# Reordering layer 0's products in the second slot and moving the next element's left sums to the third

## The chip, the cores and the metric

The kernel runs on one NeuronCore of a Trainium2 chip. The metric is the device time of one execution in microseconds (us), the median of several. The names in the profile: PE is TensorE's matmuls and PEld its weight loads, DVE is VectorE, ACT is ScalarE, POOL is GpSimd, SP is the engine that issues the DMAs. L547 is line 547 of the kernel before.

## The reference

For each of 64 elements (256 rows of 512 numbers, fp32), two layers one after the other, each with a residual and a layer norm:

```python
# layer 0: a graph layer
mi = x @ Wi.T;  mj = x @ Wj.T                 # W = [Wi | Wj]
x = layernorm(x + deg * (mi + b) + a @ mj)    # a = adjacency (256 x 256), deg = its row sums
# layer 1: attention over the graph, 8 heads of 64
q, k, v = x @ Wq.T + bq, x @ Wk.T + bk, x @ Wv.T + bv
scores = where(adj == 0, -inf, q @ k.T / 8)
x = layernorm(x + (softmax(scores) @ v) @ Wo.T + bo)
```

## The kernel before

**Products.** The two weight products of layer 0 and the four of layer 1 are done with seven block products in place of eight (a Strassen-like scheme). Its left operands are four quarters of the input and four sums or differences of them (S1 to S4, "left sums", made by `left_steps`, lines 477 to 480); its right operands are quarters of the weights and their differences, made once. For layer 0 `l0_steps(b)` returns the work of element b as a list: seven products `step1` to `step7` (called first to seventh product here, `p[0]` to `p[6]` in the lists), then the product with the graph (`neighbours`), then the layer norm and the transfer of the result (`take`, `give`, `send_h`). A product is two matmuls in the program, four in the records, onto one PSUM bank. Some products share a bank: x takes the first and third, y the fourth and sixth, z the fifth and seventh.

- Product 4 goes to y; VectorE reads it and makes u2 = y + u1 (L542).
- Product 5 goes to z; ScalarE copies z to half of mj (L547).
- Product 6 adds into y; VectorE makes u3 = y + u1 (L551); GpSimd adds u3 to that half of mj (L552), and `split` makes hi (ScalarE, L524) and lo (GpSimd, L525) of it. VectorE also adds deg * u3 to the residual (L520).
- Product 7 adds into z, so it may not start before ScalarE's copy of z is over; VectorE makes the other half of mj from z and u2 (L561), which is split in the same way.

**Elements and slots.** Two elements (b1, b2) make a group. The main loop runs 31 times; in a pass the attention of group g is interleaved with layer 0 of group g+1. `layer0(g + 1)` returns seven lists, `work[0]` to `work[6]`, and the loop runs each at a place of its own between the attention's products; the diff's "second slot" is `work[1]`, its "third slot" `work[3]`, behind the scores of head pair 5. In order of time, a pass is: `work[0]`; values of head pairs 0 and 1, their denominators (`divide_two`: den and the reciprocal rden, L882), scores of 2 and 3, **`work[1]`**; values of 2 and 3, denominators, scores of 4, `work[2]` (the graph product of b1), scores of 5, **`work[3]`**; values of 4 and 5, denominators, scores of 6 and 7, `work[4]` (products 4 to 7 of b2); values of 6 and 7, and the output and query/key/value products.

After each scores product VectorE adds the mask (L805), ScalarE takes the exponential (L809), and GpSimd adds the halves for the denominators (L812).

**What sets the order.** Matmuls, and all that stands in `in_order(...)`, are pinned behind what was written before them on the same engine; the rest is placed by the framework's scheduler, by program order where it expects the inputs to be ready. The left sums of layer 0 (`sum_x`) are pinned; the mask addition, the scaled additions L520 and the reciprocal L882 aren't. The four left sums of an element share one buffer (xS, one copy), so those of b2 can be written only when product 7 of b1 has read S4. The banks of layer 0's products and of den come from one pool of three.

Of the kernel before, what the change touches and what calls it, by code (L numbers as in the profile page):

```python
# [9 lines left out]
F32R = mybir.dt.float32r  # L10
I32 = mybir.dt.int32
AF = mybir.ActivationFunctionType
ALU = mybir.AluOpType
# [3 lines left out]
P = 128  # L17
# [207 lines left out]
def unshifted_path(ctx, tc, flag, x, adj, wiT, wjT, b0, wqT, bq, wkT, bk, wvT, bv, woT, bo, out):  # L225
# [16 lines left out]
    nc = tc.nc  # L242
    B, N, D = x.shape
    NT = N // P
# [12 lines left out]
    p1 = ctx.enter_context(tc.tile_pool(name="p1", bufs=1))  # L257
# [11 lines left out]
    def bank(name):  # L269
        return ps_m.tile([P, 512], F32, tag="mm", name=name)  # L270

    def score_banks(name):
        return ps_s.tile([P, 2, 512], F32, tag="sc", name=name)
# [8 lines left out]
    def in_order(ins):  # L282

        tc.keep_in_program_order(ins)
# [4 lines left out]
    def matmul(*args, **kw):  # L289
        in_order(nc.tensor.matmul(*args, **kw))  # L290
# [160 lines left out]
    def norm_stats(t, order=anywhere):  # L451
        st = small.tile([P, 6], F32, tag="st", name="st")
        order(nc.vector.bn_stats(st, t))
        mv = small.tile([P, 2], F32, tag="mv", name="mv")
        nc.vector.bn_aggr(mv, st)
        ve = small.tile([P, 1], F32, tag="ve", name="ve")
        nc.vector.tensor_scalar(ve, mv[:, 1:2], EPS, None, ALU.add)
        below = small.tile([P, 1], F32, tag="below", name="below")
        order(nc.vector.tensor_scalar(below, mv[:, 0:1], -1.0, None, ALU.mult))  # L459
        rstd = small.tile([P, 1], F32, tag="rstd", name="rstd")  # L460
        nc.gpsimd.tensor_tensor(rstd, ve, mhalf, ALU.pow)  # L461
        return below, rstd

    def norm_apply(t, below, rstd, order=anywhere):
        shift = small.tile([P, 1], F32, tag="shift", name="shift")
        order(nc.scalar.activation(shift, below, AF.Identity, scale=rstd))  # L466
        order(nc.scalar.activation(t, t, AF.Identity, bias=shift, scale=rstd))  # L467
# [34 lines left out]
    def l0_steps(b):  # L502
        banks, k = {}, {}

        def product(name, left, n, first):
            if first:
                banks[name] = bank("po")
            for c in range(2):
                matmul(banks[name], left[:, c, :], w0[:, n, c, :], start=(first and c == 0),
                                 stop=(c == 1), skip_group_check=True)  # L510

        def raw(t, h):
            return xT[b][:, 2 * h:2 * h + 2, t * P:(t + 1) * P]

        def keeper(name):
            k[name] = p3.tile([P, D], F32, tag="lu", name=name)
            return k[name]

        def add_scaled(t, src):
            nc.vector.scalar_tensor_tensor(xh[b][:, t, :], src, deg[:, t:t + 1], xh[b][:, t, :],  # L520
                                           ALU.mult, ALU.add)

        def split(t):
            nc.scalar.copy(k["hi"][:, t, :], k["mj"][:, t, :])  # L524
            nc.gpsimd.tensor_tensor(k["lo"][:, t, :], k["mj"][:, t, :], k["hi"][:, t, :].bitcast(F32),  # L525
                                    ALU.subtract)

        def step1():
            product("x", raw(0, 0), B11, True)
            nc.scalar.copy(keeper("u1"), banks["x"])  # L530

        def step2():
            product("w", raw(1, 1), T4, True)
            add_scaled(1, banks["w"])

        def step3():
            product("x", raw(0, 1), B21, False)
            add_scaled(0, banks["x"])

        def step4():  # L540
            product("y", xS[b]["S2"], T2, True)
            nc.vector.tensor_add(keeper("u2"), banks["y"], k["u1"])  # L542

        def step5():
            product("z", xS[b]["S1"], T1, True)
            k["mj"] = p1.tile([P, NT, D], F32, tag="mj", name="mj")
            nc.scalar.copy(k["mj"][:, 1, :], banks["z"])  # L547

        def step6():
            product("y", xS[b]["S3"], T3, False)  # L550
            nc.vector.tensor_add(keeper("u3"), banks["y"], k["u1"])  # L551
            nc.gpsimd.tensor_tensor(k["mj"][:, 1, :], k["mj"][:, 1, :], k["u3"], ALU.add)  # L552

            k["hi"] = p1.tile([P, NT, D], F32R, tag="hi", name="hi")
            k["lo"] = p1.tile([P, NT, D], F32R, tag="lo", name="lo")
            split(1)
            add_scaled(1, k["u3"])

        def step7():
            product("z", xS[b]["S4"], B22, False)  # L560
            nc.vector.tensor_add(k["mj"][:, 0, :], banks["z"], k["u2"])  # L561
            split(0)

        stats = {}

        def neighbours():
            k["pa"] = score_banks("pa")
            for i in (1, 0):
                for n, (j, part) in enumerate((j, part) for j in (1, 0) for part in ("hi", "lo")):
                    matmul(k["pa"][:, i, :], graph[:, j, i * P:(i + 1) * P], k[part][:, j, :],  # L570
                           start=(n == 0), stop=(n == 2 * NT - 1))

        def take(t):
            r = xh[b][:, t, :]
            in_order(nc.vector.tensor_add(r, k["pa"][:, t, :], r))
            stats[t] = norm_stats(r, in_order)

        def give(t):
            norm_apply(xh[b][:, t, :], *stats[t], in_order)


        return [step1, step2, step3, step4, step5, step6, step7, neighbours, lambda: take(1), lambda: take(0),
                lambda: give(1), lambda: send_h(b, 1), lambda: give(0), lambda: send_h(b, 0)]

# [10 lines left out]
    def send_h(b, t):  # L595
        i = b % NB
        if t == 1:
            h_cols[b] = dram.tile([D // P, N, P], F32, tag=f"h{i}", name="h_cols")
        nc.sync.dma_start(out=h_cols[b][:, t * P:(t + 1) * P, :].rearrange("q p n -> p q n"),
                          in_=xh[b][:, t, :].rearrange("p (q n) -> p q n", n=P))  # L600
        if t == 0:
            hB[b] = p1.tile([P, N // R, P], F32, tag="hB", name="hB")
            nc.sync.dma_start(out=hB[b].rearrange("p a n -> p (a n)"),
                              in_=h_cols[b].rearrange("q (r a) n -> (q r) (a n)", r=R))
# [63 lines left out]
    def second_late(steps):  # L668
        return [steps[0], steps[2], steps[1], *steps[3:]]
# [30 lines left out]
    def qk_steps(g, store, tag, bias, diff, early=False):  # L700

        def new_store():
            store[g] = p1.tile([P, NC, NB * N], F32, tag=tag, name=tag)

        def place(i, j):
            return store[g][:, 2 * j:2 * j + 2, i * N:(i + 1) * N]

        def biased(b):
            def evict(dst, ps):
                for m in range(2):  # L710
                    nc.scalar.activation(dst[:, m, :], ps[:, m, :], AF.Identity, bias=b[:, m:m + 1], scale=1.0)  # L711
            return evict

        def last(dst, ps, addend):
            for m in range(2):
                nc.vector.scalar_tensor_tensor(dst[:, m, :], ps[:, m, :], diff[:, m:m + 1],
                                               addend[:, m, :], ALU.add, ALU.add)

        return qkv_steps(g, True, new_store, place, biased(bias), biased(diff), last, early)
# [175 lines left out]
    def layer0(g):  # L895

        b1, b2 = NB * g, NB * g + 1

        def item(f, *args):
            return lambda: f(*args)  # L900

        p, q = l0_steps(b1), l0_steps(b2)
        return [p[:3] + [item(turn_x, b2)] + p[3:4],
                p[4:7] + [item(sum_x, b2), item(add_bias, b2)] + q[:1],
                p[7:10], p[10:] + q[1:3],
                q[3:6] + [item(turn_h, b1)] + q[6:7],
                q[7:], [item(turn_h, b2)]]

# [4 lines left out]
    def with_output_bias(g, k):  # L913
        return [*k[:2], lambda: add_output_bias(NB * g), k[2], lambda: add_output_bias(NB * g + 1), *k[3:]]

    def order_of(name):
        return [(name, n) for n in RIGHT]

    for g in range(-1, NG - 1):
        o, q, k, v = (order_of(name) for name in ("wo", "wq", "wk", "wv"))  # L920
# [18 lines left out]
    p, q = l0_steps(0), l0_steps(1)  # L939
# [19 lines left out]
    k = second_late(qk_steps(0, kT, "kT", bk_sb, bkd, True))  # L959
# [22 lines left out]
    for g in range(NG - 1):  # L982
# [20 lines left out]
        q = second_late(qk_steps(g + 1, qT, "qT", bq_sb, bqd))  # L1003
        k = second_late(qk_steps(g + 1, kT, "kT", bk_sb, bkd, True))
# [7 lines left out]
        k = with_output_bias(g + 1, k)[2:]  # L1012
# [101 lines left out]
```

## Time and profile before

The median of 3 runs is 3117.14 us (3116.6 to 3118.32); the profiled execution has a span of 3113.4 us at a granted TensorE clock of 0.999.

| engine | busy us | share of the span |
|---|---|---|
| PE (matmul) | 3071.3 | 99% |
| PEld (weight loads) | 2117.8 | 68% |
| DVE | 2148.5 | 69% |
| POOL | 1520.8 | 49% |
| ACT | 1007.8 | 32% |

A row of the order in time gives the start (us into the span), the length, engine, line, operation, what is written and read, the shapes, how many instructions the row merges, and in brackets how long the engine had been idle and what ended that. "issue" there means that the engine waited for nothing that the profile shows. In the list of waits a row gives who waited for whom, the total in us, how often, and the longest. A matmul's end is modelled, so a gap on TensorE is better read from the starts of its weight loads.

### The profile page before, as it was taken

The page shows a single profiled execution, that of the slowest core. Times are in us where ns is not written, and L with a number is a line of the kernel's source. Part 1 is how long each engine was busy: PE and PEld are TensorE (multiplying, and loading weights), DVE is VectorE, ACT ScalarE, POOL GpSimd, SP SyncE. Part 2 cuts the span into 40 slices and gives each one's busy share as a digit, 9 for nine tenths or more (in the row PEclk, how much of TensorE's full clock was granted, in tenths as well). Part 3 has the DMA queues.
Part 4 walks back from the last instruction along what each step waited for, and adds up shares of the span by engine and source line. Part 5 has one row for each costly group of instructions (what it writes and reads, how often), then busy time and mean ns, then how long its engine had stood idle before and what let it go on. Part 6 is the DMA issues. An engine that isn't in the chain of part 4 may idle for free. (4 is left out here: it accounts for less than half of the span.)

```text
span 3113.4 us, 42777 instructions
## 1 busy us (share of the span) xinstructions
PE 3071.3 (99%) x14598; PEld 2117.8 (68%) x14598; DVE 2148.5 (69%) x3234; ACT 1007.8 (32%) x1925; POOL 1520.8 (49%) x1255
## 2 busy tenths in 40 slices
PE   7999999999999999999999999999999999999998
PEld 5667766677766677666776667766677766677665
DVE  6776676766777667676667676667766667767665
ACT  2333333323333333333233332333333333323332
POOL 2544445544545445454454554454544546445453
PEclk9999999999999999999999999999999999999999
DMA  7345544455444555445553445544455444555333
GB/s 256 121 143 156 166 124 134 128 157 165 141 124 123 157 166 152 117 131 149 157 166 118 131 134 157 165 139 123 127 155 169 146 118 127 154 162 160 116 111 98
DMA packets 410395, 447.28 MB, mean 144 GB/s; under 512 B 40896, under 2 KB 300224, under 8 KB 409792
## 3 DMA queue, kind: packets, MB, share of 16 engines
q1 hardware_dynamic: 410176, 444.50, 48.3%
q8 instruction: 120, 1.97, 0.3%
q14 instruction: 99, 0.81, 0.1%
HBM read 340.79 MB, written 70.25 MB: 132 GB/s over the span
## 5 line engine op out<-in xcount | busy, mean ns | idle before, releaser
L461 POOL TENSOR_TENSOR rstd<-ve,mhalf 128x1 f32<-128x1 f32 x256 | 140.6, 554 | 724.3 <-DVE below L459 724.3
L812 POOL TENSOR_TENSOR pk<-pe 128x512 f32<-128x512 f32 x256 | 322.3, 1275 | 341.0 <-ACT pe L809 341.0
L290 PE MATMUL po<-w,xS 128*128 128x512 f32 x1024 | 470.4, 602 | 6.1 <-ACT mj L547 5.6
L290 PE MATMUL st<-hS,factor 128*128 128x256 f32 x2048 | 452.7, 379 | 1.2 <-DVE u L685 1.2
L290 PEld LDWEIGHTS st<-hS,factor 128*128 128x128 f32 x2048 | 388.4, 190 | 55.1 <-DVE u L685 1.6
L809 ACT ACTIVATE pe<-pe 128x1024 f32<-128x1024 f32 x256 | 270.8, 1058 | 379.2 <-DVE pe L805 379.2
L290 PE MATMUL st<-hT,factor 128*128 128x256 f32 x1536 | 360.7, 381 | 9.0 <-ACT u L711 8.4
L290 PE MATMUL po<-w,xT 128*128 128x512 f32 x768 | 352.3, 601 | 13.8 <-DVE xT L485 11.3
L290 PEld LDWEIGHTS po<-w,xS 128*128 128x128 f32 x1024 | 186.8, 190 | 252.2 <-issue 191.5
L290 PEld LDWEIGHTS st<-hT,factor 128*128 128x128 f32 x1536 | 289.0, 190 | 61.5 <-ACT u L711 20.8
L805 DVE TENSOR_TENSOR pe<-ps,maskT 128x1024 f32<-128x1024 f32 x256 | 297.8, 1194 | 35.3 <-PE ps L290 35.3
L882 DVE RECIPROCAL rden<-den 128x256 f32<-128x256 f32 x127 | 222.8, 1754 | 73.7 <-PE den L290 68.2
L290 PEld LDWEIGHTS po<-w,xT 128*128 128x128 f32 x768 | 143.9, 191 | 181.4 <-issue 163.0
L290 PE MATMUL ps<-qT,kT 64*128 64x256 f32 x2048 | 264.9, 392 | 0.0
L883 POOL TENSOR_TENSOR rtot<-rtot,rden 128x256 f32<-128x256 f32 x127 | 92.8, 730 | 330.2 <-DVE rden L882 330.2
L290 PE MATMUL pav<-pe,v_sb 128*64 128x256 f32 x2048 | 250.1, 386 | 1.9 <-ACT pe L809 1.8
L740 DVE TENSOR_TENSOR xh<-st,xh 128x512 f32<-128x512 f32 x186 | 144.5, 777 | 149.7 <-PE st L290 149.7
L290 PEld LDWEIGHTS pav<-pe,v_sb 128*64 128x64 f32 x2048 | 135.2, 136 | 154.2 <-issue 72.0
L290 PEld LDWEIGHTS ps<-qT,kT 64*128 64x128 f32 x2048 | 184.3, 186 | 78.2 <-issue 51.3
L290 PE MATMUL st<-factor,hS 128*128 128x256 f32 x1024 | 234.8, 382 | 0.0
L290 PE MATMUL st<-factor,oS 128*128 128x256 f32 x992 | 224.2, 379 | 0.0
L290 PEld LDWEIGHTS st<-factor,hS 128*128 128x128 f32 x1024 | 191.9, 190 | 35.4 <-issue 10.6
(115 smaller groups left out, 4657.0 us busy)
## 6 DMA issues: line engine op xcount, KB each, us to landing
xB<-in_x_dram SPq DMA_DIRECT2D x256, 128.0 KB, 3.9
xh<-in_x_dram SPq DMA_DIRECT2D x64, 512.0 KB, 4.4
factor<-wq SPq DMA_DIRECT2D x128, 256.0 KB, 4.4
factor<-wk SPq DMA_DIRECT2D x128, 256.0 KB, 2.7
factor<-wv SPq DMA_DIRECT2D x128, 256.0 KB, 2.7
spread<-rden SPq DMA_DIRECT2D x1016, 32.0 KB, 1.9
factor<-wo SPq DMA_DIRECT2D x124, 256.0 KB, 3.3
h_cols<-xh SPq DMA_DIRECT2D x124, 256.0 KB, 2.5
```

Of the source, the lines that this page charges most:

```text
L290: in_order(nc.tensor.matmul(*args, **kw))
L461: nc.gpsimd.tensor_tensor(rstd, ve, mhalf, ALU.pow)
L740: nc.vector.tensor_add(dst, src, dst)
L805: nc.vector.tensor_add(pe.rearrange("p j t q -> p j (t q)"), ps.rearrange("p j t q -> p j (t q)"), maskT.rearrange("p t q -> p (t q)").uns ...
L809: in_order(nc.scalar.activation(flat, flat, AF.Exp, scale=QSCALE, accum_out=etot[:, NB * g + i, pr:pr + 1]))
L812: nc.gpsimd.tensor_tensor(pk, pe[:, :, 0, :], pe[:, :, 1, :], ALU.add)
L882: nc.vector.reciprocal(rden, den)
L883: nc.gpsimd.tensor_tensor(rtot, rtot, rden, ALU.add)
```

## The change

The second slot ran products 5, 6 and 7 of b1, then the left sums of b2, the addition of the bias to b2's residual, and b2's first product. Now it runs products 6 and 5 of b1, b2's first product, and product 7 of b1, then the bias. So two products instead of one stand between product 5 and product 7, for ScalarE's copy of z to be over. As u3 and mj's half can now be ready in either order, the addition of the two and the split stand in a helper, `join`, which does them in whichever of step5 and step6 comes second. The left sums of b2, which need product 7 of b1 to be over, move to the third slot, behind b1's layer norm and ahead of b2's second and third products. The startup, which runs the steps in an order of its own, keeps its order.

```diff
+        def join(*needed):
+            if all(n in k for n in needed):
+                nc.gpsimd.tensor_tensor(k["mj"][:, 1, :], k["mj"][:, 1, :], k["u3"], ALU.add)
+
+                k["hi"] = p1.tile([P, NT, D], F32R, tag="hi", name="hi")
+                k["lo"] = p1.tile([P, NT, D], F32R, tag="lo", name="lo")
+                split(1)
+
         def step5():
             product("z", xS[b]["S1"], T1, True)
             k["mj"] = p1.tile([P, NT, D], F32, tag="mj", name="mj")
             nc.scalar.copy(k["mj"][:, 1, :], banks["z"])
+            join("u3")
 
         def step6():
             product("y", xS[b]["S3"], T3, False)
             nc.vector.tensor_add(keeper("u3"), banks["y"], k["u1"])
-            nc.gpsimd.tensor_tensor(k["mj"][:, 1, :], k["mj"][:, 1, :], k["u3"], ALU.add)
-
-            k["hi"] = p1.tile([P, NT, D], F32R, tag="hi", name="hi")
-            k["lo"] = p1.tile([P, NT, D], F32R, tag="lo", name="lo")
-            split(1)
+            join("mj")
             add_scaled(1, k["u3"])
...
         return [p[:3] + [item(turn_x, b2)] + p[3:4],
-                p[4:7] + [item(sum_x, b2), item(add_bias, b2)] + q[:1],
-                p[7:10], p[10:] + q[1:3],
+                [p[5], p[4], q[0], p[6], item(add_bias, b2)],
+                p[7:10], p[10:] + [item(sum_x, b2)] + q[1:3],
                 q[3:6] + [item(turn_h, b1)] + q[6:7],
                 q[7:], [item(turn_h, b2)]]
```

## The prediction

> **What bounds the kernel now.** I read the page's busy times, then the list of waits, then the order in time of one main-loop pass (1441 to 1537 us into the span; a pass takes 96.0 us, and 31 are alike).
>
> ```profile
> PE 3071.3 (99%) x14598; PEld 2117.8 (68%) x14598; DVE 2148.5 (69%) x3234; ACT 1007.8 (32%) x1925; POOL 1520.8 (49%) x1255
> ```
>
> TensorE sets the end: 99% busy, nearest other engine 69%. A change can save only what stands between TensorE's products, or cost by opening a new gap there. The list of waits names one gap in the stretch that the diff touches:
>
> ```profile
> PEld po L290 <- ACT mj L547: 31.3, 31, 1.0
> ...
> PE po L290 <- ACT mj L547: 5.6, 31, 0.2
> ```
>
> Once per pass a weight load of a layer-0 product waits for the copy of z into mj. In order of time, second slot:
>
> ```profile
> 1453.22 1.06 ACT L809 ACTIVATE pe<-pe 128x1024 f32<-128x1024 f32 x1
> ...
> 1453.69 0.19 PEld L290 LDWEIGHTS po<-w,xS 128*128 128x128 f32 x1 [0.24 <-issue]
> ...
> 1454.28 0.56 ACT L547 COPY mj<-po 128x512 f32<-128x512 f32 x1
> ...
> 1454.89 0.30 PEld L290 LDWEIGHTS po<-w,xS 128*128 128x128 f32 x2 [1.01 <-ACT mj L547]
> ```
>
> Products 5, 6, 7 run in that order. Product 7 adds into z's bank, so it waits until ScalarE has copied product 5 out; the copy stands behind the exponential of the scores just before. Loads otherwise come 0.43 us apart; here 1454.89 - 1453.69 = 1.20. The load after it comes 0.11 later (0.30 for two less 0.19 for one), then 0.43 each: four loads take 1.20 + 0.11 + 0.43 + 0.43 = 2.17 where 4 x 0.43 = 1.72 would do. **The stall is 0.45 us**, though the matmul row admits only 0.18. The load was 0.77 late and cost 0.45, so a load may be 0.32 late at no cost.
>
> **What the Trainium skill says.** "Perfetto Trace Analysis", Identifying the Most-Contended Engine: matmul busy time doesn't show how near TensorE is to its best, and bubbles that recur on the saturated engine are what to look for. The trace agrees: 99% busy, and the same 0.45 us in every pass. "PSUM — Partial Sum Buffer", Terms: two engines may not be in one bank at once; the load indeed comes 0.05 us after the copy (1454.28 + 0.56 to 1454.89). "SBUF — State Buffer", SBUF: two separate sides: a VectorE operation with two SBUF inputs and a GpSimd operation exclude each other, each for the whole instruction. The trace agrees, in slot 2:
>
> ```profile
> 1458.22 2.72 POOL L525 TENSOR_TENSOR lo<-mj,hi 128x512 fp32r<-128x512 f32 x2 [0.73 <-ACT hi L524]
> 1458.32 1.50 DVE L479 TENSOR_TENSOR xS<-xT 128x256 f32<-128x256 f32 x1
> ...
> 1459.73 1.50 DVE L480 TENSOR_TENSOR xS<-xT,xS 128x256 f32<-128x256 f32 x1
> ...
> 1461.15 1.75 DVE L882 RECIPROCAL rden<-den 128x256 f32<-128x256 f32 x1
> ```
>
> The third and fourth left sums take 1.50 each beside GpSimd's two subtractions; the same sums with GpSimd idle take 0.42 and follow 0.34 apart:
>
> ```profile
> 1432.98 0.41 DVE L479 TENSOR_TENSOR xS<-xT 128x256 f32<-128x256 f32 x1
> 1433.32 0.42 DVE L480 TENSOR_TENSOR xS<-xT,xS 128x256 f32<-128x256 f32 x1
> ```
>
> **Part 1, the new order 6, 5, next element's 1, 7.** Same instructions, so no busy time is added. Product 7's load would fall due 5 x 0.43 after 1453.69, at 1455.84. Product 5 is now second and ends where 6 did, when VectorE's u3 addition could start (1454.75); the exponential is over by then (1454.28), so the copy runs to about 1455.3: 0.5 us to spare. The next element's first product takes product 7's old place, load due at 1454.12. It needs a bank, at worst the one that u3's addition frees: that addition moves up behind the two mask additions, about 1453.2, and ends at 1453.9. No wait. The join (mj + u3) still starts when both are there and GpSimd is done with the score sums (1455.78 before; up to 0.6 later and 0.45 shorter now, since the scaled u3 addition, which slowed it to 1.72, falls before it). Product 7's addition comes 1.3 later, but the subtractions queue on GpSimd and end near 1460.9 as now, over 1 us ahead of the graph products. So **-0.45 per pass, 31 x 0.45 = -13.9 us**. The stall of the second element's own product 7 (slot 4) doesn't exist: its copy idled 0.38 for TensorE.
>
> **Part 2, the left sums out of slot 2.** There they hid under TensorE, except that the fourth ends at 1461.23 and holds up the next reciprocal: it starts 0.75 after its den load (1460.40), the others 0.70 to 0.71. **-0.04 per pass, -1.2 us**, since this reciprocal, the mask addition and the next score products follow one another without slack.
>
> **Part 3, the left sums in slot 3.** This is the cost. VectorE there, before:
>
> ```profile
> 1466.62 1.21 DVE L805 TENSOR_TENSOR pe<-ps,maskT 128x1024 f32<-128x1024 f32 x1
> ...
> 1468.35 0.73 DVE L520 SCALAR_TENSOR_TENSOR xh<-po,deg,xh 128x512 f32<-128x512 f32 x1
> ...
> 1469.09 1.28 POOL L812 TENSOR_TENSOR pk<-pe 128x512 f32<-128x512 f32 x1 [1.98 <-ACT pe L809]
> ...
> 1469.34 0.74 DVE L520 SCALAR_TENSOR_TENSOR xh<-po,deg,xh 128x512 f32<-128x512 f32 x1
> 1470.33 0.55 POOL L461 TENSOR_TENSOR rstd<-ve,mhalf 128x1 f32<-128x1 f32 x1
> ...
> 1471.39 1.76 DVE L882 RECIPROCAL rden<-den 128x256 f32<-128x256 f32 x1 [1.31 <-PE den L290]
> ```
>
> VectorE is busy from 1464.2 to 1470.08 and has only that 1.31 us of slack ahead of the reciprocal. The sums are pinned behind the mask addition of 1466.62, with the two scaled additions (L520) and the reciprocal behind them. In the times of before: after the statistics (1467.75 to 1468.35) the first sum at 1468.35; the small aggregation at 1468.69; the second sum at 1468.80; two small ones; the third asks at 1469.28. GpSimd's score sum began at 1469.09 and holds the ports to 1470.37. In slot 2 the third sum ended 0.3 after the GpSimd operation that blocked it; so here 1470.67, the fourth from 1470.59, the scaled additions at 1470.93 and 1471.58 (0.65 each), the reciprocal at 1472.23 instead of 1471.39, 0.84 late. What follows it:
>
> ```profile
> 1473.06 2.29 DVE L805 TENSOR_TENSOR pe<-ps,maskT 128x1024 f32<-128x1024 f32 x2
> ...
> 1475.27 0.68 DVE L542 TENSOR_TENSOR u<-po,u 128x512 f32<-128x512 f32 x1
> ...
> 1476.29 0.19 PEld L290 LDWEIGHTS po<-w,xS 128*128 128x128 f32 x1 [0.24 <-issue]
> ```
>
> Reciprocal, two mask additions and the u2 addition follow without a gap: 1475.95 - 1471.39 = 4.56. u2 now ends at 1472.23 + 4.56 = 1476.79. The load at 1476.29 opens the second element's product 6, which adds into the bank that u2's addition reads, so it comes at 1476.84, 0.55 late, of which 0.32 is free: **+0.23 per pass, +7.1 us**. Products 4 and 5 need the scaled additions' banks and the first two sums, there by 1472.3, ahead of 1473.18 and 1474.9: nothing.
>
> The unknown is how often the sums meet GpSimd. Lower bound: never; they take 1.36, beside 1.31 + 0.61 of slack: 0. Upper: one more full GpSimd operation, 1.2 more: 1.43. The small L461 next to the fourth sum I take at nothing, for in the startup it waited for one VectorE subtraction and the next was not slowed (0.68 both):
>
> ```profile
> 42.81 0.99 POOL L461 TENSOR_TENSOR rstd<-ve,mhalf 128x1 f32<-128x1 f32 x1 [2.68 <-DVE below L459]
> 43.31 0.68 DVE L417 TENSOR_TENSOR t<-raw,t 128x512 f32<-128x512 f32 x1
> ```
>
> **Sum:** -0.45 - 0.04 + 0.23 = -0.26 per pass, x 31 = -8.1: **3109.0 us**. Startup runs neither the new slot nor the moved sums: nothing.
>
> **Rivals.**
> - Full gain: the sums fit in the slack. For it: 1.36 is less than 1.92. Against: the score sum sits right on the third. -0.49 x 31 = -15.2: 3101.9.
> - L461 does hold the ports, 0.45 more: +0.68 - 0.49 = +0.19, +5.9: 3123. Against: the one case above.
> - Slower: the sums meet two full GpSimd operations (the second sum comes 0.3 later than I place it and loses to the score sum, or the fourth meets the multiplication behind L461). +1.43 - 0.49 = +0.94, +29: 3146. For: 0.3 us separates them.
> - The stall comes back in slot 2 at the first product or 7, and the cost is hidden: about 3117. Against: margins of 0.2 and 0.5.
>
> **Chances.** Forecast 0.46, full gain 0.17, L461 0.15, two meetings 0.12, stall kept 0.10. The forecast case spreads by 5 us, so a third of it falls within 0.2% (6.2 us) of before: faster 0.30 + 0.17 = 0.47; same 0.15 + half of L461 + most of stall kept = 0.28; slower 0.25. Range 3100 to 3127: from the full gain to L461, leaving out the two meetings and the edges.
>
> **What would show it.** Right: no wait of po on mj L547, loads in slot 2 0.43 apart; the third left sum about 1.4 long in slot 3, the fourth short; the reciprocal of slot 4 some 0.8 later behind the den products; a new wait of po for DVE u L542, 31 times. Wrong: if the scaled additions come ahead of the sums, if two sums are stretched, or if the reciprocal still idles for den.

## The result and the profile after

The changed kernel takes 3132.87 us (median of 4, 3132.18 to 3134.47) where the kernel before took 3117.0: ratio 1.0051, 95% interval 1.0033 to 1.0068. It is slower by 15.9 us, 0.51 us for each of the 31 passes. (Behind the helper, which stands at line 544, the line numbers of the new file are 5 to 9 higher: the copy of z is L555, u3 is L560, the mask addition L810, the exponential L814, the score sum L817, the multiplication of the values by their spread inverses L849, the reciprocal L887. The addition of mj and u3 is L546.)

The stall at product 7 is gone. The weight loads of the second slot, in order of time, end of product 5 to product 7:

```profile
1460.76 0.19 PEld L290 LDWEIGHTS po<-w,xS 128*128 128x128 f32 x1 [0.24 <-issue]
1461.19 0.19 PEld L290 LDWEIGHTS po<-w,xT 128*128 128x128 f32 x1 [0.24 <-issue]
...
1462.47 0.19 PEld L290 LDWEIGHTS po<-w,xT 128*128 128x128 f32 x1 [0.24 <-issue]
1462.90 0.19 PEld L290 LDWEIGHTS po<-w,xS 128*128 128x128 f32 x1 [0.24 <-issue]
```

Four products run at 0.43 us a load without a break. The list of waits has a new entry in its place:

```profile
PEld po L290 <- DVE u L542: 47.6, 31, 1.5
...
PE po L290 <- DVE u L542: 21.9, 31, 0.7
```

That is product 6 of the second element, in slot 4 (`work[4]`), waiting for the addition of u2:

```profile
1482.47 0.19 PEld L290 LDWEIGHTS po<-w,xS 128*128 128x128 f32 x1 [0.24 <-issue]
1484.20 0.30 PEld L290 LDWEIGHTS po<-w,xS 128*128 128x128 f32 x2 [1.54 <-DVE u L542]
```

The load comes 1.73 after the one before it instead of 0.43, 1.30 late; with 0.32 free, that is a stall of 0.98. The sums of a pass, from the starts of weight loads (medians over 30 passes, us; a slot runs from its first load to the first load of the values behind it), show nothing else that moved:

| | slot 2 | slot 4 | whole pass |
|---|---|---|---|
| before | 7.51 | 7.06 | 95.98 |
| after | 7.06 | 8.04 | 96.50 |

So -0.45 + 0.98 = +0.53, and the pass grew by 0.52. Where the 0.98 comes from stands in the third slot; VectorE and GpSimd there, in order of time:

```profile
1474.96 0.41 DVE L477 TENSOR_TENSOR xS<-xT 128x256 f32<-128x256 f32 x1
1475.29 0.18 DVE L455 BATCH_NORM_AGGREGATE mv<-st 128x2 f32<-128x6 f32 x1
1475.38 0.72 DVE L520 SCALAR_TENSOR_TENSOR xh<-po,deg,xh 128x512 f32<-128x512 f32 x1
...
1475.71 1.28 POOL L817 TENSOR_TENSOR pk<-pe 128x512 f32<-128x512 f32 x1 [1.78 <-ACT pe L814]
...
1476.13 1.14 DVE L478 TENSOR_TENSOR xS<-xS,xT 128x256 f32<-128x256 f32 x1
...
1476.95 1.45 POOL L849 TENSOR_TENSOR aoT<-aoT,spread 128x512 f32<-128x512 f32 x1
1477.19 1.49 DVE L479 TENSOR_TENSOR xS<-xT 128x256 f32<-128x256 f32 x1
...
1477.30 0.64 PE L290 MATMUL den<-pk,ones 128*32 128x256 f32 x8
...
1478.61 0.41 DVE L480 TENSOR_TENSOR xS<-xT,xS 128x256 f32<-128x256 f32 x1
1478.94 0.74 DVE L520 SCALAR_TENSOR_TENSOR xh<-po,deg,xh 128x512 f32<-128x512 f32 x1
...
1479.60 1.74 DVE L887 RECIPROCAL rden<-den 128x256 f32<-128x256 f32 x1
...
1481.27 2.28 DVE L810 TENSOR_TENSOR pe<-ps,maskT 128x1024 f32<-128x1024 f32 x2
...
1483.47 0.67 DVE L542 TENSOR_TENSOR u<-po,u 128x512 f32<-128x512 f32 x1
```

Two sums are stretched, not one. The second (L478) takes 1.14 instead of 0.42, since the score sum (L817) began 0.42 ahead of it; the third (L479) takes 1.49, behind the multiplication (L849). The reciprocal starts 2.30 after the den products' start; before it was 1471.39 - 1470.68 = 0.71. It is 1.59 late. The mask additions and u2 follow it without a gap; u2 ends at 1484.14, and the load at 1484.20 is the one that waited.

### The profile page after: what moved, and what is told of

Same layout as the page of the kernel before. It is cut to its first block, busy times and chain, and to the rows that moved or that the text cites. A ratio compares the mean times of both kernels' runs of the same rounds, so it can differ in the third digit from the quotient of the medians.

```text
span 3130.3 us, 42776 instructions
## 1 busy us (share of the span) xinstructions
PE 3071.7 (98%) x14598; PEld 2117.9 (68%) x14598; DVE 2141.3 (68%) x3234; ACT 1007.7 (32%) x1925; POOL 1520.8 (49%) x1255
## 5 line engine op out<-in xcount | busy, mean ns | idle before, releaser
L817 POOL TENSOR_TENSOR pk<-pe 128x512 f32<-128x512 f32 x256 | 336.3, 1329 | 334.6 <-ACT pe L814 334.5
L461 POOL TENSOR_TENSOR rstd<-ve,mhalf 128x1 f32<-128x1 f32 x256 | 146.4, 576 | 724.3 <-DVE below L459 724.3
L814 ACT ACTIVATE pe<-pe 128x1024 f32<-128x1024 f32 x256 | 270.8, 1058 | 378.7 <-DVE pe L810 378.7
L810 DVE TENSOR_TENSOR pe<-ps,maskT 128x1024 f32<-128x1024 f32 x256 | 297.8, 1193 | 35.1 <-PE ps L290 35.1
L887 DVE RECIPROCAL rden<-den 128x256 f32<-128x256 f32 x127 | 222.7, 1753 | 88.9 <-PE den L290 83.1
```

The costliest lines, as they stand in the source:

```text
L810: nc.vector.tensor_add(pe.rearrange("p j t q -> p j (t q)"), ps.rearrange("p j t q -> p j (t q)"), maskT.rearrange("p t q -> p (t q)").uns ...
L814: in_order(nc.scalar.activation(flat, flat, AF.Exp, scale=QSCALE, accum_out=etot[:, NB * g + i, pr:pr + 1]))
L817: nc.gpsimd.tensor_tensor(pk, pe[:, :, 0, :], pe[:, :, 1, :], ALU.add)
L887: nc.vector.reciprocal(rden, den)
```

## The experiments

Three theories are compared. *Ports*: the new product order gains 0.45 a pass, and the moved left sums cost what they cost because they wait for GpSimd operations. *Order*: the new product order itself costs. *Own time*: the sums cost by their own length and place, whatever GpSimd does. "Before" in each ratio is the kernel before, on the same chip.

**The moved sums alone, with the old product order.**

```diff
-                p[4:7] + [item(sum_x, b2), item(add_bias, b2)] + q[:1],
-                p[7:10], p[10:] + q[1:3],
+                p[4:7] + [item(add_bias, b2)] + q[:1],
+                p[7:10], p[10:] + [item(sum_x, b2)] + q[1:3],
```

> The product order of before (5, 6, 7, next element's first), with the left sums in the third slot as in the changed kernel. Port theory (the gain of the new product order is there, 0.45 us a pass, and the moved left sums cost 0.97 a pass because two of them wait for GpSimd operations that hold the shared SBUF ports): stall at product 7 kept, cost of the sums whole, -0.05 for the earlier reciprocal of slot 3: +0.92 x 31 = +28.5, 3145.5 us, with product 6 of the second element waiting 1.5 us for u2. Order theory (the new product order is what costs, the moved sums are hidden): about 3117 or a little less.

Measured: 3148.1 us, ratio 1.0098 (1.0082 to 1.0113). Both stalls stand side by side in the list of waits:

```profile
PE po L290 <- DVE u L542: 21.7, 31, 0.7
...
PE po L290 <- ACT mj L547: 5.7, 31, 0.2
```

Slot 2 takes 7.51 as before, slot 4 8.03, the pass 96.96. Against the changed kernel (96.50) only the product order differs: it is worth 0.46 a pass. The order theory is out, and the moved sums alone cost 0.98.

**The new order, left sums at the end of slot 2.**

```diff
-                [p[5], p[4], q[0], p[6], item(add_bias, b2)],
-                p[7:10], p[10:] + [item(sum_x, b2)] + q[1:3],
+                [p[5], p[4], q[0], p[6], item(sum_x, b2), item(add_bias, b2)],
+                p[7:10], p[10:] + q[1:3],
```

> The new product order, with the left sums at the end of the second slot, behind product 7, where the shared buffer forces them. Port theory: VectorE reaches them at about 1465.9 in the times of the changed kernel, beside GpSimd's two subtractions, the bias addition and a multiplication; each sum waits for one of these, the last ends near 1472 where the reciprocal was due at 1467.7, and the mask addition and the next score products follow it without slack: about +4 a pass, 3117 - 14 + 125 = about 3230 us. Own-time theory (only the sums' own 1.4 us count): they would end at 1467.3, ahead of the reciprocal, and cost nothing: about 3103.

Measured: 3314.96 us, ratio 1.0635 (1.0619 to 1.0651). The third and fourth sum, the two GpSimd operations that they wait for, and the score products at the end of the chain:

```profile
1448.45 2.56 POOL L374 TENSOR_TENSOR xh<-xh,degb 128x1024 f32<-128x1024 f32 x1
1448.69 2.60 DVE L479 TENSOR_TENSOR xS<-xT 128x256 f32<-128x256 f32 x1
...
1450.97 1.45 POOL L849 TENSOR_TENSOR aoT<-aoT,spread 128x512 f32<-128x512 f32 x1
1451.21 1.48 DVE L480 TENSOR_TENSOR xS<-xT,xS 128x256 f32<-128x256 f32 x1
...
1455.49 2.08 PE L290 MATMUL ps<-qT,kT 64*128 64x256 f32 x8 [4.20 <-DVE pe L810]
```

All four sums wait (the first two take 0.99 and 1.38); TensorE stands 4.2 us. The two shown each ask 0.24 us after a GpSimd operation has begun and end just under 0.3 after it: four short sums among GpSimd operations pay for most or all of one each, one after another. That much was expected ("about +4 a pass"; the score products come 4.27 later behind the graph products than in the kernel before). The rest, 2.60 a pass, wasn't: after the pause these products and the two behind them run slower (see the last section). Own time, which forecast 3103, is out.

**The new order, with two buffers for the left sums.** The sums of b2 then needn't wait for product 7 of b1, and go in the second slot where VectorE idles for it.

```diff
-            xS[b] = left_blocks(a11, a12, a21, a22, p1.tile([P, 4, 2, P], F32, tag="xS", name="xS"))
+            xS[b] = left_blocks(a11, a12, a21, a22, p2.tile([P, 4, 2, P], F32, tag="xS", name="xS"))
...
-                [p[5], p[4], q[0], p[6], item(add_bias, b2)],
-                p[7:10], p[10:] + [item(sum_x, b2)] + q[1:3],
+                [p[5], p[4], item(sum_x, b2), q[0], p[6], item(add_bias, b2)],
+                p[7:10], p[10:] + q[1:3],
```

> The new product order, with a second buffer for the left sums, so that they stand in the second slot between the two products of which VectorE reads the first (6) and product 7, in 3.0 us in which VectorE idles. Nothing is added to the third slot. Port theory: gain of the order whole and no cost: -0.50 x 31 = -15.4, 3101.7 us; product 7's addition up to 0.6 later, which nothing waits for. Order theory: the order itself costs, 3117 or more.

Measured: 3101.7 us, ratio 0.9952 (0.9939 to 0.9966), faster than both kernels. VectorE in its second slot:

```profile
1448.85 1.48 DVE L477 TENSOR_TENSOR xS<-xT 128x256 f32<-128x256 f32 x1
...
1450.37 1.37 DVE L478 TENSOR_TENSOR xS<-xS,xT 128x256 f32<-128x256 f32 x1
...
1452.33 0.68 DVE L566 TENSOR_TENSOR mj<-po,u 128x512 f32<-128x512 f32 x1
...
1454.44 1.76 DVE L887 RECIPROCAL rden<-den 128x256 f32<-128x256 f32 x1 [1.44 <-PE den L290]
```

Two sums are stretched by GpSimd here too (1.48 and 1.37), and it costs nothing: the reciprocal still idles 1.44 for den. Slot 2 takes 7.06, slot 4 7.06, the pass 95.54.

**The changed kernel with the order that the forecast assumed.** The scaled addition of product 2 is pinned behind the sums (`add_scaled` now returns its instruction; those lines aren't shown).

```diff
             product("w", raw(1, 1), T4, True)
-            add_scaled(1, banks["w"])
+            in_order(add_scaled(1, banks["w"]))
```

> The changed kernel with the scaled addition of the second element's product 2 pinned behind the left sums. VectorE's order in the third slot is then the one that the forecast assumed: statistics, first sum, aggregation, second sum, two small ones, third and fourth sum, both scaled additions. If the forecast failed only because the scheduler put the scaled addition between the first and second sum: the second sum again beats GpSimd's score sum, one meeting in place of two, reciprocal 0.84 late, product 6 stalls 0.23: 3109 us. If the sums cost whatever their place: 3133.

Measured: 3109.82 us, ratio 0.9977 (0.9968 to 0.9986). The third slot:

```profile
1465.47 0.41 DVE L477 TENSOR_TENSOR xS<-xT 128x256 f32<-128x256 f32 x1
1465.79 0.17 DVE L455 BATCH_NORM_AGGREGATE mv<-st 128x2 f32<-128x6 f32 x1
1465.91 0.42 DVE L478 TENSOR_TENSOR xS<-xS,xT 128x256 f32<-128x256 f32 x1
...
1466.21 1.27 POOL L817 TENSOR_TENSOR pk<-pe 128x512 f32<-128x512 f32 x1 [1.78 <-ACT pe L814]
...
1466.38 1.39 DVE L479 TENSOR_TENSOR xS<-xT 128x256 f32<-128x256 f32 x1
...
1467.44 0.73 POOL L461 TENSOR_TENSOR rstd<-ve,mhalf 128x1 f32<-128x1 f32 x1
1467.69 0.41 DVE L480 TENSOR_TENSOR xS<-xT,xS 128x256 f32<-128x256 f32 x1
...
1469.34 1.74 DVE L887 RECIPROCAL rden<-den 128x256 f32<-128x256 f32 x1
```

The second sum starts 0.3 ahead of the score sum and takes 0.42; one sum is stretched. L461 also runs ahead of the multiplication again, so the fourth sum met only L461, and wasn't slowed. The reciprocal starts 1.54 after the den products (1467.80), 0.83 late; slot 4 takes 7.28, a stall of 0.22, and no other stretch of the pass moved. Same sums, same slot, same work: 23 us less than the changed kernel.

**The changed kernel with the multiplication put off** behind slot 4's score sums, VectorE's order untouched.

```diff
             values(g, w - 1)
+            held = []
+            if w == 6:
+                held, products[:] = products[:], []
             multiply()
...
             later()
+            fresh, products[:] = products[:], held or products[:]
+            if held:
+                multiply()
+                products.extend(fresh)
```

> The changed kernel, with the multiplication of the values by their spread inverses (GpSimd, aoT<-aoT,spread) that opens slot 4 put behind the score sums of that slot. VectorE's order stays that of the changed kernel, so the second left sum still meets the score sum, but the third no longer meets the multiplication. Port theory: 1.07 a pass less on VectorE, reciprocal 0.5 late instead of 1.6, inside the slack of 0.61 ahead of product 6, no stall: -0.50 x 31, 3101.7 us. If the sums cost by their own length and place: 3133 as before.

Measured: 3106.88 us, ratio 0.9969 (0.9957 to 0.9981). The second sum still waits, the third no longer:

```profile
1464.37 1.14 DVE L478 TENSOR_TENSOR xS<-xS,xT 128x256 f32<-128x256 f32 x1
...
1465.43 0.41 DVE L479 TENSOR_TENSOR xS<-xT 128x256 f32<-128x256 f32 x1
...
1466.76 1.74 DVE L887 RECIPROCAL rden<-den 128x256 f32<-128x256 f32 x1
```

The reciprocal is 0.52 late, and slot 4 takes 7.06: no stall, as expected. Most of the 5 us that it misses against 3101.7 are elsewhere:

```profile
PE st L290 <- ACT u L716: 12.2, 31, 0.5
```

This wait was 8.4 in the kernel before. In the products behind the second element's graph product one load comes 0.13 later (7.69 us after the first of them, for 7.56 before; medians over 30 passes), 4 us in 31 passes. In order of time, the multiplication now runs ahead of the second element's mj + u3 on GpSimd, whose chain up to the layer norm ends 0.12 later; ScalarE scales late, and its query and key copies queue behind. That this chain is the cause is read from the trace; no run tests it alone.

**Both together.**

> Both: scaled addition pinned behind the sums, and the multiplication put off. Port theory: the third sum meets the score sum, the fourth nothing; the multiplication already met nothing in this order, so no gain over the pinned version: 3110 us. If putting off the multiplication helps by itself (less to wait for elsewhere): 3102 or less.

Measured: 3117.0 us, ratio 1.0 (0.9991 to 1.0008), against 3110 expected. Slot 4 takes 7.28 (stall 0.22, as expected), but the load behind the late GpSimd chain now comes 0.25 later (7.81 for 7.56), twice as much as in the run before. The expectation had taken putting off as free.

**The left sums behind products 2 and 3.**

```diff
-                p[7:10], p[10:] + [item(sum_x, b2)] + q[1:3],
+                p[7:10], p[10:] + q[1:3] + [item(sum_x, b2)],
```

> The changed kernel with the left sums behind the second element's products 2 and 3, so that VectorE does both scaled additions first and the sums last. Port theory: the first sum asks at 1476.6 in the times of the changed kernel and waits for the score sum (to 1477.0), the second slips in, the third waits for the multiplication to about 1479.1, reciprocal 1.65 late: +0.54 a pass, 3134 us. If only the position of the scaled addition between the first two sums cost: 3109.

Measured: 3127.81 us, ratio 1.0038 (1.0026 to 1.005). The third slot:

```profile
1475.39 1.28 POOL L817 TENSOR_TENSOR pk<-pe 128x512 f32<-128x512 f32 x1 [1.78 <-ACT pe L814]
...
1476.29 0.67 DVE L477 TENSOR_TENSOR xS<-xT 128x256 f32<-128x256 f32 x1
...
1477.34 1.54 POOL L849 TENSOR_TENSOR aoT<-aoT,spread 128x512 f32<-128x512 f32 x1
...
1477.67 1.49 DVE L480 TENSOR_TENSOR xS<-xT,xS 128x256 f32<-128x256 f32 x1
```

The first sum meets the end of the score sum, the second and third slip in, and the fourth, not the third, meets the multiplication. The reciprocal is 1.39 late where 1.65 was expected, and slot 4 takes 7.84, a stall of 0.78 where 1.04 was expected: between the forecasts, nearer to that of the ports. Doing both scaled additions first doesn't save the sums from GpSimd.

## Why the prediction was wrong

**Right.** Part 1 holds to the hundredth: 0.45 a pass, no new wait at the next element's first product or at product 7, and the join on GpSimd in time (its subtractions end 0.71 ahead of the graph products, not "over 1 us": the prediction left out that these come 0.45 earlier too). The kind of chain that costs is right as well: left sums held up by GpSimd operations, reciprocal late, mask additions and u2 behind it without a gap, product 6 stalled, with 0.61 of slack (0.52 late in the run with the multiplication put off: no stall; 0.83: 0.22; 1.59: 0.98).

**The step that failed** is "the small aggregation at 1468.69; the second sum at 1468.80" in Part 3, with "the two scaled additions (L520) and the reciprocal behind" the four sums. The scaled additions aren't pinned, and the trace of before shows the scheduler placing one of them between two instructions of which the second needs the first (1468.35, between the statistics and the aggregation). The forecast took them in program order. In the built kernel the first sum stands where it was forecast, but behind the aggregation comes a scaled addition (1475.38) and only then the second sum, so this asks 0.4 us after the score sum has begun, not 0.3 ahead of it. It waits. The small instruction that feeds L461 (L457) is late as well, the multiplication runs ahead of L461, and the third sum meets the multiplication. Two meetings in place of one: the term priced at +0.23 measured +0.98. With the forecast's order pinned in the code the same term measured +0.22, and the kernel 3109.8 us for 3109.0.

Why the multiplication runs first is argued, not shown: where L457 starts up to 0.12 us after the score sum (before, the pinned order, the sums last) L461 goes first, and where it starts 0.3 after it (the changed kernel, the moved sums alone) the multiplication does.

The rival "two meetings" named this outcome, mechanism and margin (0.3 us), and got a chance of 0.12. Its price, +1.43, was too high: the second sum was held 0.72, not a full operation's 1.2, as part of the score sum had run while the scaled addition did. The range ended at 3127 and left this case out, though only 0.3 us spoke against it, in an order that no row of before showed.

**A small term wrong.** The -0.04 of Part 2 didn't come. In the run with two buffers the reciprocal is on time (0.71 after den), yet the next score products come 0.55 after the last graph product as before. The 0.37 that stands before them in the list, "DVE pe", is no stall.

**L461 at nothing** was right: 0.41 for the sum beside it.

The Trainium skill's "SBUF — State Buffer", SBUF: two separate sides, calls the port pair that VectorE and GpSimd share an exclusive lock for the whole instruction. The runs agree for large operations (a sum of 0.42 takes 1.4 to 1.5 behind a GpSimd operation of 1.3, and 2.60 behind one of 2.56), and not for L461, a GpSimd instruction on one number a row: beside a sum it took 0.73 instead of 0.54 us, and the sum ran in its usual 0.41. Where they differ, the measurement decides.

## What to carry to other kernels

- Removing a bubble on the bound engine is worth just that bubble; what the edit pushes elsewhere is priced by the slack of the place where it lands. In the third and fourth slot VectorE had 1.92 us a pass (1.31 ahead of the reciprocal and 0.61 ahead of product 6), and the sums put off the work behind them by 2.90 (1.31 + 1.59).
- Where VectorE operations with two SBUF inputs stand among GpSimd operations, their cost depends on who asks first. The second sum took 0.42 where it asked 0.3 us ahead of a GpSimd operation, and 1.14 where it asked 0.4 behind. Put them where VectorE waits for something anyway, even if that takes a second buffer: 4 KB a partition turned a loss of 0.5% into a gain of 0.5%.
- Where a scheduler orders what isn't pinned, an order that the forecast rests on should be pinned in the code or counted as unknown.

## What the runs showed of the hardware that was not expected

In the kernel with the sums at the end of slot 2 TensorE's granted clock fell in its pause of 4.2 us, in every pass, and stayed down for some 5 us behind it. The stretches of one pass, with the granted clock in the third column from the right:

```profile
1440.00:1451.00 11.00, 11.00 (x54) 5.58 (x52) 7.89 (x7) 4.83 (x9) 9.27 (x7) 1.00 0.12 33
1451.00:1455.50 4.50, 0.30 (x3) 0.01 (x2) 4.50 (x5) 0.03 (x1) 2.14 (x3) 0.84 0.00 0
1455.50:1459.00 3.50, 3.50 (x10) 2.01 (x11) 3.40 (x8) 1.13 (x3) 1.77 (x2) 0.50 0.21 56
1459.00:1463.00 4.00, 4.00 (x9) 1.44 (x9) 1.72 (x6) 2.21 (x5) 1.93 (x3) 0.77 0.26 75
1463.00:1480.00 17.00, 17.00 (x95) 9.52 (x92) 11.03 (x10) 6.81 (x12) 9.99 (x9) 1.00 0.24 67
```

At a clock of 0.50 the score products took 2.01 instead of 1.06 and the two products behind them 5.28 instead of 3.63: 2.60 a pass on top of the pause. The Trainium skill's "TensorE: Matmul & The Clock Gate", HAM oscillation, says this of pauses over some 3.4 us, and the trace agrees with its 4.2; stalls of up to 0.98 us in the main loop of the other kernels left the mean clock at 0.999. What a pause between the two does was not tested. So the pause, which put these products off by 4.27 us, cost another 60% of that.
